# Four chained layers on one core: layer 0's settling by quarters of the tokens, and the end of layer 2 beside the start of layer 3

## The chip, the core and the metric

The kernel runs on one core of a Trainium2 chip. A core has five engines that work side by side and wait for each other by semaphores: TensorE (PE in the profile, with its weight loads listed apart as PEld), which multiplies matrices into the PSUM memory; VectorE (DVE), for arithmetic over rows and reductions; ScalarE (ACT), for functions such as Exp, Tanh and Gelu, of which it holds some in a table and has to load another table for others; GpSimd (POOL); and SyncE (SP), which here only issues DMA transfers. Each engine works through its own queue in the order in which the program puts it. On-chip memory is SBUF, 128 partitions wide.

The metric is the device time of one execution in microseconds (us).

## The reference

The input is x, 8 sequences of 512 tokens with 128 features (f32). Four layers follow, and each is

```
xn = layernorm(x)
s  = attention_i(xn, ...)
g  = silu(ffn_i(xn, ...))
x  = x + s * g
```

Layer 0's "attention" is a recurrence with 16 heads of 8 features. Per token it updates an 8x8 state S for each head, reads y from it, and normalizes y over the 8 features of the head:

```
S = S*exp(w)[:, None] + (S @ kk)[:, None]*b + v[:, None]*k ;  y = S @ r
yn = (y - mean(y)) / sqrt(var(y) + 0.00064) * ln_w + ln_b
out = ((yn + (sum(r*k*faaaa))*v) * g) @ output.T
```

Its ffn is a mixture of 48 experts, each of which takes its 128 best tokens. Layer 1 is an attention over a Taylor feature map with a mixture of 8 experts. Layer 2 has causal softmax attention (16 heads), then eight steps of a small recurrence over the whole sequence,

```
u = tanh(ctx @ w_ctx + xs @ w_x + b);  vn = vs + 0.1*(u - xs - vs);  xs = xs + 0.1*vn
```

then a Gelu block, and a separate gated ffn of width 512. Layer 3's "attention" is a state-space mixer: parameters (decays, rotations, mixing weights) from a projection, and then chunks of tokens in order. Its ffn slot holds an attention with 16 heads whose softmax goes over the queries, followed by two normalized projections.

## The kernel before

A tile holds 128 rows (P). A sequence of 512 tokens has JT = 4 token tiles, and there are B = 8 sequences. `blocks` runs `layer0` to `layer3` one after the other, and x stays in SBUF throughout. Python generators express work that is spread among other work: each `yield` ends a piece, and whoever holds the generator calls `next` to emit the next piece.

**Who sets the order.** By default a planner orders each engine's instructions by estimated readiness, in favour of what comes first in the program. `manual_schedule(engines=...)` takes engines out of its hands: they get their instructions exactly as the program emits them. Layers 0, 1 and 2 do so for PE alone, layer 3 for PE, DVE, ACT and POOL. Memory comes from tile pools. A tile whose memory was used by an earlier one waits until that one's last user is done.

**Layer 0.** For each of the four token tiles (`jt`), the partitions hold the 128 pairs of sequence and head, and the recurrence goes over the 128 tokens two at a time: 64 pairs of tokens, in 8 rounds of SH = 8 pairs (`o`). A round emits, in this order: an expert piece from `side`, three pieces of the next token tile's preparation (`go_on(3)`), the outputs of the round before (`outputs`: sums over 8 values on PE by `eighths` and an ACT copy into Y), another expert piece, two more pieces of preparation, and then the recurrence itself (L734 to L765), nearly all of it DVE instructions of 32 to 128 columns in two interleaved halves. After the eight rounds comes the settling for the whole token tile (L772 to L782): DVE adds the part of v that the pairing left out (L772, L773); the mean over 8 values is formed by `eighths` on PE, and DVE subtracts it (L777); ACT squares (L778); PE sums the squares; ACT takes Ln and Exp for the inverse root (L779, L780); DVE forms the bonus times v (L781) and scales Y (L782). Then ACT applies ln_w and ln_b (L784, eight instructions), PE adds and transposes (L796), DVE applies the gate (L799), and the output projection follows (L804 to L814).

**Layer 2.** It loops over 128 units (sequence, head group, key tile): weights (scores and Exp), maxima for later units, and the sums of LAG = 2 units before. Between these, `fill` emits pieces of the next sequence's start (`begin`, `ffn`), and of the finished sequences (`group`, `rest`). `group` turns the sums into outputs, and its last call for a sequence also does the output projection. `rest` does the norm, the eight recurrence steps (L1557 product with w_x, L1559 add, L1560 Tanh, L1562 to L1565 updates), and the Gelu block, and adds into x (L1603). When the loop ends, the last sequence's pieces remain, and the last two lines of `layer2` emit them with nothing beside them.

**Layer 3.** `begin(b)` normalizes a sequence and projects queries, keys and values for the ffn slot's attention, and then goes on into `parameters`, for the mixer. After `begin(0)`, up to its values, a loop goes over 8 x 16 units plus an end. A unit has `scores` (PE products L2089 into four PSUM banks, DVE maxima L2091, ACT exponentials L2094; a bank is free for the next unit once its exponential is done), `weigh` for two units before (L2119), `scale` for the unit before (the reciprocal L2105), and two calls of `fill`. `fill` gives one piece to every active mixer, and to ends and begins as long as a credit (SHARE a call) lasts. A mixer handles one token tile of one sequence (its first product is L1978). Unit `at(b, jt)` starts it: every 3 units from unit 9 on, and later every 4. If the sequence's parameters aren't complete by then, they are emitted all at once. `end(b)` does the projections behind the attention and the final sum, and issues the output DMA.

Of the kernel before, what the change touches and what calls it, by code (L numbers as in the profile page):

```python
# [20 lines left out]
P = 128  # L21
B = 8
# [308 lines left out]
def layer0(k, x, A, at):  # L331
# [5 lines left out]
    with ExitStack() as ctx:  # L337
# [355 lines left out]
        for jt in range(JT):  # L693
# [12 lines left out]
            yp = Y.rearrange("p (t s) v -> p t s v", s=2)  # L706
            last = None
            for o in range(0, HT, SH):
                if jt == JT - 1 and o // SH >= HT // SH - JT:
# [13 lines left out]
                    else:  # L723
                        held = f, old
                next(side, None)
                go_on(3)
                if last:
                    outputs(*last)
                next(side, None)
# [38 lines left out]
            outputs(*last)  # L768
            go_on(40)
            ready = made  # L770
            t3 = fp.tile([P, B, C], F32, name="EWt").rearrange("p b (h n) -> p (b h) n", n=8)
            nc.vector.tensor_tensor(t3[:, 0:HT], Vs[:, :, 0, :], bc(kr, 2, 8), ALU.mult)  # L772
            nc.vector.tensor_tensor(yp[:, :, 0, :], yp[:, :, 0, :], t3[:, 0:HT], ALU.add)  # L773


            mu = bp.tile([P, P], F32, name="mu")
            nc.vector.scalar_tensor_tensor(Y, Y, 8.0, bc(eighths(Y), 2, 8), ALU.mult, ALU.subtract)  # L777
            nc.scalar.activation(t3, Y, AF.Square)  # L778
            nc.scalar.activation(mu, eighths(t3), AF.Ln, bias=k.eps_gn, scale=1.0 / 8)  # L779
            nc.scalar.activation(mu, mu, AF.Exp, scale=-0.5)  # L780
            nc.vector.tensor_tensor(t3, Vs.rearrange("p t s n -> p (t s) n"), bc(bonus, 2, 8), ALU.mult)  # L781
            nc.vector.tensor_tensor(Y, Y, bc(mu, 2, 8), ALU.mult)  # L782
            for n in range(8):
                nc.scalar.activation(  # L784
                    Y[:, :, n], Y[:, :, n], AF.Identity, scale=cn["ln_w"][:, n : n + 1], bias=cn["ln_b"][:, n : n + 1]
                )

# [4 lines left out]
            for n0 in range(0, 8, 4):  # L792
                ps = k.pa((P, 4, P))
                for i in range(4):
                    for src in (Y, t3):
                        nc.tensor.matmul(  # L796
                            ps[:, i, :], src[:, :, n0 + i], k.ident, start=(src is Y), stop=(src is t3)
                        )
# [515 lines left out]
class Layer2(BySequence):  # L1314


    def __init__(self, k, ctx, x, A, at):
        self.k, self.x = k, x
        nc, tc = k.nc, k.tc
        pool = lambda name, bufs=1: ctx.enter_context(tc.tile_pool(name="l2" + name, bufs=bufs, reuse_waits="tile"))  # L1320
        cp = pool("c")
        self.cn = cn = k.load_consts(cp, A["c2"], at[0], "c2")
        self.fn = fn = k.load_consts(cp, A["f2"], at[1], "f2")

        self.half_s = cp.tile([P, 4], F32, name="half_s")
        nc.vector.tensor_scalar(self.half_s, fn["w1_s"], 0.5, None, ALU.mult)
        self.both_s = cp.tile([P, 4], F32, name="both_s")
# [279 lines left out]
def layer2(k, x, A, at):  # L1607

    with ExitStack() as ctx:
# [62 lines left out]
        for _ in chain(groups, rest):  # L1672
            next(front, None)
# [644 lines left out]
```

## Time and profile before

| | us |
|---|---|
| median of three runs (3601.0 to 3603.7) | 3602.8 |
| the profiled execution's own time | 3603.7 |
| its span, from first to last instruction | 3602.0 |
| layer 0's last update of x | 875.3 |
| layer 2's loop: first score | 1466.4 |
| layer 3's loop: first score | 2624.5 |

How to read the profile: a line of a stretch gives its start, end and length in us; then for PE, PEld, DVE, ACT and POOL the busy us and, in brackets, the number of instructions; then the clock that PE was granted (1 is full), the DMA engines' busy share and GB/s. A stretch for one source line has only the engine of that line. A line of the timeline gives start and duration in us, engine, line, operation, output and inputs, their shapes, and how often; in square brackets stands how long the engine had been idle, and for whom it waited. Neighbouring instructions of one kind are merged, and the duration then runs from the first's start to the last's end. An f32 product appears as two MATMUL passes, each with its own weight load.

### The profile page before, as it was taken

The numbers are of one execution on the slowest core, as the hardware profiler recorded it, in microseconds if no ns is written. First come the engines' busy times: TensorE is split into PE (matmuls) and PEld (weight loads), VectorE is DVE, ScalarE is ACT, GpSimd is POOL, SyncE is SP. The second block draws the span as 40 slices with busy tenths as digits, with TensorE's granted clock in tenths as the row PEclk, the third lists the DMA queues.
The fourth block names the chain that finished last, engine by engine and source line by source line (L and its number), as shares of the span: only waits on it lengthen the run. The fifth ranks groups of instructions, "written<-read, shape, count | busy, mean of one in ns | idle before, by whom it ended". The sixth has DMA issues, their size and how long they took to land.

```text
span 3602.0 us, 46273 instructions
## 1 busy us (share of the span) xinstructions
PE 2864.4 (80%) x16950; PEld 1575.1 (44%) x16950; DVE 2322.8 (64%) x6354; ACT 1790.3 (50%) x3382; POOL 729.9 (20%) x845
## 2 busy tenths in 40 slices
PE   6175868635988898798888898898588798888887
PEld 4154656534444454333334333443235454444443
DVE  7999888896582334435455454554368777777775
ACT  4173646412544455254454554455255565666665
POOL 0012131300225553101111111111112221212221
PEclk8587889766899999899999999999678888888888
DMA  4012121211001222000000000000000000000000
GB/s 121 2 30 44 31 52 32 43 49 34 1 13 37 39 42 47 37 1 1 1 1 1 1 1 1 1 1 1 2 20 1 4 4 3 2 4 4 4 1 7
DMA packets 67523, 64.59 MB, mean 18 GB/s; under 512 B 5344, under 2 KB 59616, under 8 KB 66784
## 3 DMA queue, kind: packets, MB, share of 16 engines
q1 hardware_dynamic: 39264, 42.75, 3.9%
q0 software_dynamic: 19712, 14.69, 3.1%
q10 hardware_dynamic: 8320, 4.19, 0.4%
q8 instruction: 133, 2.18, 0.3%
q14 instruction: 94, 0.77, 0.1%
HBM read 43.80 MB, written 17.83 MB: 17 GB/s over the span
## 4 chain that ended last, share of the span: by engine, by line
PE 34%; DVE 14%; ACT 10%; issue 2%; POOL 1%; DMA 0%; POOLq 0%; ACTq 0%; DVEq 0%; SPq 0%
PE pu L1454 6%; PE ph L1435 5%; PE pu L2089 5%; DVE nm L2091 2%; PE pf L2119 2%; ACT at L2094 2%; PE pf L1503 2%; ACT at L1490 2%; ACT L1490 1%; PE pa L1557 1%; DVE mpad L1469 1%; PE pu L1466 1%; PE pa L1580 1%; PE pa L2132 1%; PE pa L2027 1%
## 5 line engine op out<-in xcount | busy, mean ns | idle before, releaser
L2094 ACT ACTIVATE at<-pu,nm 128x512 f32<-128x512 f32 x512 | 348.0, 691 | 195.9 <-DVE nm L2091 193.4
L2091 DVE TENSOR_REDUCE nm<-pu 128x1 f32<-128x512 f32 x512 | 319.0, 682 | 90.7 <-PE pu L2089 90.6
L2089 PE MATMUL pu<-qT,kT 32*128 32x512 f32 x1024 | 285.8, 732 | 87.6 <-ACT at L2094 87.2
L199 POOL TENSOR_SCALAR_AFFINE_SELECT at<-at 128x512 f32<-128x512 f32 x184 | 125.1, 680 | 1024.4 <-ACT at L1490 878.0
L1469 DVE TENSOR_REDUCE mpad<-pu 128x2 f32<-128x1024 f32 (+3 forms) x256 | 199.0, 819 | 148.8 <-PE pu L1466 148.7
L1128 ACT ACTIVATE at<-pu,rsqrt 128x1024 f32<-128x1024 f32 (+3 forms) x256 | 191.1, 793 | 188.0 <-PE pu L1123 160.7
L1435 PE MATMUL ph<-hid,f 128*128 128x512 f32 x512 | 255.5, 626 | 11.6 <-ACT hid L1436 11.5
L1490 ACT ACTIVATE at<-pu 128x1024 f32<-128x1024 f32 (+3 forms) x256 | 167.0, 701 | 163.7 <-PE pu L1454 162.7
L364 PE MATMUL pa<-HR,ident 128*128 128x128 f32 x512 | 127.8, 418 | 140.2 <-DVE HR L765 140.2
L364 PEld LDWEIGHTS pa<-HR,ident 128*128 128x128 f32 x512 | 112.7, 265 | 150.2 <-DVE HR L765 74.6
L2089 PEld LDWEIGHTS pu<-qT,kT 32*128 32x128 f32 x1024 | 95.3, 212 | 177.9 <-ACT at L2094 162.5
L2119 PE MATMUL pf<-at,va 128*32 128x512 f32 x1024 | 165.0, 723 | 1.9 <-POOL va L2106 1.9
L608 POOL DMA_INDIRECT f_d<-ys,idx x48 | 87.8, 1828 | 384.6 <-ACT ys L607 355.1
L1454 PE MATMUL pu<-kT,qT 32*128 32x512 f32 (+3 forms) x1024 | 134.9, 500 | 30.0 <-ACT at L1490 29.2
L1454 PE MATMUL pu<-qT,kT 32*128 32x512 f32 (+3 forms) x1024 | 128.0, 492 | 20.7 <-DVE mpad L1469 20.2
L1435 PEld LDWEIGHTS ph<-hid,f 128*128 128x128 f32 x512 | 94.1, 198 | 113.2 <-issue 89.2
L2106 POOL TENSOR_TENSOR va<-V,sm 128x32 f32<-128x32 f32 x128 | 33.7, 263 | 489.0 <-DVE sm L2105 488.4
L1123 PE MATMUL pu<-qT,kT 32*128 32x512 f32 (+3 forms) x1024 | 128.4, 507 | 5.3 <-ACT at L1128 4.4
L1066 POOL DMA_INDIRECT f_d<-ys,idx x64 | 102.8, 1606 | 142.7 <-DMA f_d<-ys,idx 86.0
L1490 ACT ACT_TABLE_LOAD x66 | 84.7, 1283 | 87.8 <-PE pu L1454 87.0
L1133 DVE TENSOR_TENSOR at<-at,ceiling 128x512 f32<-128x512 f32 x72 | 49.9, 695 | 105.6 <-ACT at L1128 99.9
L691 ACT COPY Y<-pa 128x128 f32<-128x128 f32 x32 | 8.5, 265 | 208.7 <-PE pa L364 208.7
(621 smaller groups left out, 6772.5 us busy)
## 6 DMA issues: line engine op xcount, KB each, us to landing
w<-in_w_dram SPq DMA_DIRECT2D x24, 512.0 KB
f_d<-zeros ACTq DMA_DIRECT2D x8, 512.0 KB
xn_d<-xn SPq DMA_DIRECT2D x8, 512.0 KB
w<-in_w_dram SPq DMA_DIRECT2D x16, 256.0 KB
w<-in_w_dram SPq DMA_DIRECT2D x24, 128.0 KB
f<-in_f_dram SPq DMA_DIRECT2D x1, 2888.0 KB
xn<-in_x_dram SPq DMA_DIRECT2D x4, 512.0 KB
Gt<-in_x_dram SPq DMA_DIRECT2D x4, 512.0 KB
```

Source lines behind the costliest of these rows:

```text
L199: self.nc.gpsimd.affine_select(a, a if src is None else src, pattern, ALU.is_ge, 0.0, base=0, channel_multiplier=-1)
L364: nc.tensor.matmul(ps, k.ident, src[:, :, i], start=(i == 0), stop=(i == 7))
L1123: nc.tensor.matmul(pu[:, n, 0:m], q["kT"][r, g // 2, kc * P : kc * P + P], q["qT"][r, g, kc * P :], start=True, stop=True,)
L1128: nc.scalar.activation(at_[:, i : i + 2, 0:m], pu[:, :, 0:m], AF.Square, bias=k.rsqrt2, scale=32.0**-0.5)
L1435: nc.tensor.matmul(ps, fn[n][:, c0 : c0 + P], src[:, i, :], start=(i == 0), stop=(i == 3))
L1454: self.k.nc.tensor.matmul(pu[:, n, 0:m], a[r, c0 : c0 + P], b[r, q0 : q0 + m], start=True, stop=stop)
L1469: nc.vector.tensor_reduce(top[:, i : i + 2, 16 + g % 2], pu[:, :, 0:m], AX.X, ALU.max)
L1490: nc.scalar.activation(at_[:, i : i + 2, 0:m], pu[:, :, 0:m], AF.Exp, scale=8.0**-0.5)
L2089: nc.tensor.matmul(pu, q["kT"][r, kc * P : (kc + 1) * P], q["qT"][r, g, :], start=True, stop=True)
L2091: nc.vector.tensor_reduce(nm[:, n : n + 1], pu, AX.X, ALU.max, negate=True)
L2094: nc.scalar.activation(E[:, n, :], pu, AF.Exp, bias=nm[:, w], accum_out=sm[:, w])
L2119: nc.tensor.matmul(po[i * 32 : i * 32 + 32, :], va[:, kc, c0 : c0 + 32], E[:, i, :], start=(kc == 0), stop=(kc == JT - 1))
```

## The change

In layer 0 the settling, up to the scaling of Y, becomes a generator `settle(c)` for a quarter of the tokens (16 pairs, 32 tokens). Quarter c starts in the third, fifth or seventh round (c = 0, 1, 2), right after the outputs of the round before, and gives one further piece at the start of each later round. The fourth quarter, and what is left of the third, are emitted after the rounds. The bonus times v now overwrites Vs, where it had its own buffer. The ln_w scaling and all that follows stay as they were.

In layers 2 and 3, `layer2` no longer emits the last sequence's remaining pieces. It leaves them in `k.tail` with a function that frees their memory. Layer 2's pools split for this: what the tail needs (constants c2, small tiles, work tiles) lies on the right side of SBUF and stays; the ffn's weights, values, queries, keys and weights lie on the left side and are freed before layer 3. Layer 3 emits one tail piece after each piece of `begin(0)`, then one after the first half of each unit's scores, and one more at the end of every odd unit, all in its fixed order. `parameters` is separate from `begin`, with a list of its own; `parameters(0)` starts once the tail is done. Mixers start from unit 19 every 10/3 units. SHARE is 1.9. Ends come last in `fill`, one at a time, and their first projection, now `attended(b)`, is emitted with the last `weigh`. Layer 3's pools use the same `reuse_waits="tile"` as the others.

```diff
+            def settle(c, Y=Y, yp=yp, mu=mu, Vs=Vs, bonus=bonus, kr=kr):
+                pr, tk = slice(c * 16, c * 16 + 16), slice(c * 32, c * 32 + 32)
+                own_v = bp.tile([P, 16, 8], F32, name="own_v")
+                nc.vector.tensor_tensor(own_v, Vs[:, pr, 0, :], bc(kr[:, pr], 2, 8), ALU.mult)
+                nc.vector.tensor_tensor(yp[:, pr, 0, :], yp[:, pr, 0, :], own_v, ALU.add)
+                yield
+                y = Y[:, tk, :]
+                nc.vector.scalar_tensor_tensor(y, y, 8.0, bc(eighths(y), 2, 8), ALU.mult, ALU.subtract)
+                square = bp.tile([P, 32, 8], F32, name="square")
+                nc.scalar.activation(square, y, AF.Square)
+                v = Vs.rearrange("p t s n -> p (t s) n")[:, tk, :]
+                nc.vector.tensor_tensor(v, v, bc(bonus[:, tk], 2, 8), ALU.mult)
+                yield
+                nc.scalar.activation(mu[:, tk], eighths(square), AF.Ln, bias=k.eps_gn, scale=1.0 / 8)
+                nc.scalar.activation(mu[:, tk], mu[:, tk], AF.Exp, scale=-0.5)
+                nc.vector.tensor_tensor(y, y, bc(mu[:, tk], 2, 8), ALU.mult)
+                yield
+
+            settling = []
...
+                for works in settling:
+                    next(works, None)
                 next(side, None)
                 go_on(3)
                 if last:
                     outputs(*last)
+                    if o // SH % 2 == 0:
+                        settling.append(settle(o // SH // 2 - 1))
+                        next(settling[-1])
...
             outputs(*last)
+            settling.append(settle(3))
             go_on(40)
             ready = made
-            t3 = fp.tile([P, B, C], F32, name="EWt").rearrange("p b (h n) -> p (b h) n", n=8)
-            nc.vector.tensor_tensor(t3[:, 0:HT], Vs[:, :, 0, :], bc(kr, 2, 8), ALU.mult)
-            nc.vector.tensor_tensor(yp[:, :, 0, :], yp[:, :, 0, :], t3[:, 0:HT], ALU.add)
...
-            nc.vector.scalar_tensor_tensor(Y, Y, 8.0, bc(eighths(Y), 2, 8), ALU.mult, ALU.subtract)
-            nc.scalar.activation(t3, Y, AF.Square)
-            nc.scalar.activation(mu, eighths(t3), AF.Ln, bias=k.eps_gn, scale=1.0 / 8)
-            nc.scalar.activation(mu, mu, AF.Exp, scale=-0.5)
-            nc.vector.tensor_tensor(t3, Vs.rearrange("p t s n -> p (t s) n"), bc(bonus, 2, 8), ALU.mult)
-            nc.vector.tensor_tensor(Y, Y, bc(mu, 2, 8), ALU.mult)
+            for step in chain(*settling):
+                pass
...
 def layer2(k, x, A, at):
+    late = ExitStack()
...
-        for _ in chain(groups, rest):
-            next(front, None)
+        assert next(front, None) is None
+        k.tail = chain(groups, rest), late.close
...
 def layer3(k, x, A, at):
...
-        SHARE = 1.75
-        EARLY, EVERY = 9, 3
-        at = lambda b, jt: max(b * U + jt * JT - 2, EARLY + EVERY * (b * JT + jt))
-        mixers, begins, ends = [], [L.begin(0)], []
-        while not L.q or "ready" not in L.q[0]:
-            next(begins[0])
+        SHARE = 1.9
+        EARLY, EVERY = 19, 10 / 3
+        at = lambda b, jt: max(b * U + jt * JT - 2, EARLY + int(EVERY * (b * JT + jt)))
+        mixers, begins, parameters, ends = [], [], [], []
+        tail, release = k.tail
+        for _ in L.begin(0):
+            next(tail, None)
...
-            for works in (mixers, ends, begins):
-                for w in works[:1] if works is begins else list(works):
+            for works in (mixers, begins, parameters, ends):
+                for w in list(works) if works is mixers else works[:1]:
...
+                if b and n == b * U - 1:
+                    whole(begins)
+                if b and n == max((b - 1) * U + 8, at(b - 1, JT - 1) + 1 - U, at(b - 2, JT - 1) + 1 if b > 1 else 0):
+                    while "V" not in L.q.get(b, ()):
+                        next(begins[0])
+                    parameters.append(L.parameters(b))
             scores = L.scores(*divmod(n, U)) if n < B * U else iter(())
             next(scores, None)
+            if tail and next(tail, False) is False:
+                tail = None
+                release()
+                L.more_pools()
+                parameters.append(L.parameters(0))
             fill()
             next(scores, None)
             if LAG <= n < B * U + LAG:
-                L.weigh(*divmod(n - LAG, U))
+                b, u = divmod(n - LAG, U)
+                L.weigh(b, u)
+                if u == U - 1:
+                    assert not tail
+                    L.attended(b)
+                    ends.append(L.end(b))
             if 1 <= n <= B * U:
                 L.scale(*divmod(n - 1, U))
+            if tail and n % 2:
+                next(tail, None)
             fill()
```

## The prediction

> **What bounds the kernel now.** I read the page first, then a table of stretches, then the timeline of the two seams that the change touches. The page:
>
> ```profile
> span 3602.0 us, 46273 instructions
> ...
> DVE  7999888896582334435455454554368777777775
> ...
> PEclk8587889766899999899999999999678888888888
> ```
>
> A slice is 90 us. In layer 0 (slices 3 to 9) VectorE (DVE) is at 9 of 10: the recurrence is a chain on it. In layers 1 and 2 TensorE (PE) is the busy engine. At slice 29, the seam from layer 2 to 3, DVE and the granted clock both dip. The stretches (busy us of PE, PEld, DVE, ACT and POOL, then the clock):
>
> ```profile
> 708.00:839.00 131.00, 50.82 (x227) 46.04 (x227) 121.55 (x680) 22.26 (x39) 7.22 (x8) 0.64 0.14 34
> 839.00:875.30 36.30, 24.72 (x104) 22.61 (x104) 9.49 (x13) 11.19 (x17) 3.64 (x7) 0.68 0.02 2
> 2470.00:2544.00 74.00, 61.09 (x352) 28.33 (x350) 31.14 (x51) 41.72 (x53) 9.28 (x13) 0.93 0.00 1
> 2544.00:2624.50 80.50, 39.51 (x108) 17.74 (x108) 33.00 (x59) 14.02 (x21) 8.06 (x9) 0.64 0.06 23
> 2690.60:2960.60 270.00, 232.32 (x1323) 134.12 (x1322) 209.41 (x467) 162.82 (x432) 67.13 (x98) 0.87 0.01 3
> 2960.60:3546.70 586.10, 503.85 (x2733) 265.85 (x2733) 443.89 (x1018) 367.57 (x966) 125.88 (x197) 0.85 0.01 3
> ```
>
> Row 1 is layer 0's last token tile: DVE does 121.6 of 131 us, so a DVE instruction put there costs its own time. Row 2 is what follows it, 36 us in which no engine is full. Row 4 is the tail of layer 2's last sequence: 80.5 us of pure latency from its last sums to layer 3's first score. The timeline shows one of its eight recurrence steps:
>
> ```profile
> 2564.22 0.69 DVE L1565 SCALAR_TENSOR_TENSOR X<-X,u 128x512 f32<-128x512 f32 x1 [0.79 <-ACT u L1560]
> 2564.94 0.69 DVE L1564 SCALAR_TENSOR_TENSOR X<-X,X 128x512 f32<-128x512 f32 x1
> 2564.96 0.50 PEld L1557 LDWEIGHTS pa<-X,c 128*128 128x128 f32 x2 [3.84 <-DVE X L1565]
> 2564.96 2.08 PE L1557 MATMUL pa<-X,c 128*128 128x512 f32 x2 [2.26 <-DVE X L1565]
> 2567.08 0.69 DVE L1559 TENSOR_TENSOR u<-pa,cw 128x512 f32<-128x512 f32 x1 [1.44 <-PE pa L1557]
> 2567.86 0.72 ACT L1560 ACTIVATE u<-u,c 128x512 f32<-128x512 f32 x1 [3.68 <-DVE u L1559]
> ```
>
> One step is 4.40 us (2564.96 to 2569.36), of which every engine is free for half or more.
>
> Layer 3 is a loop over 128 units (one head group against one key tile), in an order that the program fixes on four engines. One reciprocal (L2105) per unit counts them:
>
> ```profile
> 2690.60:2960.60 270.00, 5.57 (x33) 0.87 0.01 3
> 2960.60:3546.70 586.10, 13.34 (x79) 0.85 0.01 3
> ```
>
> The first stretch holds 33 units and 11 mixers (one every 3 units; counted by L1978, two passes each), the second 79 units and 20 mixers (one every 4). If a unit costs b and a mixer with its share of begin, parameters and end costs m: 33b + 11m = 270.0 and 79b + 20m = 586.1, so b = 5.0 and m = 9.5 us. This pair carries the sum below.
>
> **Layer 0, the settling by quarters.** Removed per token tile: five DVE instructions, 2 x 0.69 (128x512) + 3 x 1.23 (128x1024) = 5.1 us. Added: 20, per quarter two of 128x128 and three of 128x256. The nearest rows are 0.29 (L1522) and 0.42 (L1593): 1.84 a quarter, 7.4 a tile, +2.3. Back to back, starts lie closer than durations (two of 128x64 in 0.35, not 2 x 0.22), which makes the difference +1.0; I take +1.6. TensorE's two sums over the eight values become eight of a quarter of the columns; each still loads weights 16 times, 3.66 to 3.77 us at the low clock, so about 3.7 instead of 4.1 each. PE's 80 idle us of row 1 cover the 22 us that a tile gains (eight of 3.7 less two of 4.1); if PE is late, DVE waits at each sum. POOL and SP get nothing here. ACT gets four times the Ln and Exp. The last tile's end:
>
> ```profile
> 844.21 4.12 PE L364 MATMUL pa<-Y,ident 128*128 128x128 f32 x16 [1.08 <-DVE Y L773]
> 848.36 1.22 DVE L777 SCALAR_TENSOR_TENSOR Y<-Y,pa 128x1024 f32<-128x1024 f32 x1 [4.21 <-PE pa L364]
> 850.75 1.28 ACT L779 ACT_TABLE_LOAD   x1
> 850.78 4.00 PE L364 MATMUL pa<-EWt,ident 128*128 128x128 f32 x16 [2.46 <-ACT EWt L778]
> 855.21 1.28 ACT L780 ACT_TABLE_LOAD   x1
> ```
>
> Here row and rule differ. The Trainium skill's "ScalarE: Activation LUTs" (Table sets: the hidden batching unit) says that a logarithm followed by an exponential needs one table load, since one set has both, and (What ACT_TABLE_LOAD costs) that a switch is 2.66 us, load and drain. The trace has two loads, of 1.28 each, with Exp starting 0.01 us after the second. By the rule a quarter pays one switch of 2.66 us, and 5.3 with the way back to Gelu or Tanh, and the exposed end would lose 1.3 us. I go by the row: 2 x 1.28 a quarter and one load back, 3.8 us. ACT is idle 109 us of row 1; earlier tiles have it half busy, and there a late Ln can push the next tile's front.
>
> Inner tiles (three): +1.6 of DVE; the two DVE waits for the sums (L777 2.03, L781 2.03 at 361 and 368) lose one, since the bonus product no longer overwrites the squares, -2.0; new waits of DVE on PE or ACT inside the recurrence, unseen before, bounded by none and by two of 2.0 per quarter: I take +1.0. That is +0.6 each, +1.8. Last tile: three quarters inside its full DVE, at 1.4 us with overlap, +4.2. Its end from 843.5 to 858.1 shrinks: add 0.69 to 0.29, sums 8.1 to 7.4, subtraction 1.22 to 0.42, square 1.06 to 0.4, scale 1.23 to 0.42, -3.7 with the smaller Ln and Exp; but the third quarter's variance sum now stands before it on PE, 3.7 less the 1.1 that PE idled there: +2.6. The eight ACT scalings and what follows stay. So -1.1, and layer 0 is +1.8 + 4.2 - 1.1 = **+5 us** (from -8, all six waits gone and no new one, to +18, one more wait of 2 us per quarter in half of them).
>
> **Layer 2 into layer 3.** The layer 2 loop keeps its order; its tiles only change place. Its first loads may go earlier or later than 1435 and 1443 us, but what ends last there is the sum into x on POOL (to 1447.6): 0, within 3.
>
> The start of layer 3. Its constants (1313 and 514 KB) fall where layer 2's ffn weights lay, last read at about 2520; their 7 us (issue 2609.8, first use 2616.8) end before 2544, SP being idle. If an overlap delays them past 2544, each us counts. begin(0) took 14.5 us by itself (2610.0 to 2624.5). Now its nine pieces alternate with nine of the tail: four that finish the attention, the norm, X, and three recurrence steps. Before, those reached 2571.5. The tail leads, and begin's two 2-us products, Wk and Wq, and two qT scalings of 0.75 fall into it, while a busier PE shortens the product from 2.08 to the 1.12 that it had at 2509.5. I put the first scores at 2569 instead of 2624.5: **-55.5**.
>
> The first eight units. Twelve calls remain, 1.5 a unit. A unit with a step runs: scores 0.6, four maxima 2.5, u 0.7, Tanh 0.8, two exponentials 1.4, hand-overs 0.5, some 6.5; a second step adds some 3 to 4; the last norm adds 6, the two Gelu pieces 4 each with 2 x 1.28 of loads, begin(1) some 5. Summed: 5.5 + 12 + 6 + 12 + 5 + 11 + 5.5 + 7.5 = 65. Bare they would be 40. What is late behind the tail on ACT are the unit's third and fourth exponentials, on PE the next scores that need their banks.
>
> The rule that speaks against this is in "TensorE: Matmul & The Clock Gate" (Architectural detail): ScalarE's and VectorE's queues are strictly first in, first out. Read at its hardest, each of the 12 calls adds its whole latency: 8 x 5.0 + 12 x 4.4 = 93 us. The trace agrees in kind: at 2672 the parameters' sine waits 0.77 and loads tables twice around a unit's exponentials, and that unit takes 7.5. But most of a step's 4.4 passes while DVE does the unit's maxima. I take 65 and keep 93 for the range.
>
> The rest. Units 8 to 18: parameters(0), moved here, at the 6.2 us that nine units had with it before (2635.3 to 2690.8): 68. Units 19 to 121 hold 31 mixers, one per 10/3 units: 103 x 5.0 + 31 x 9.5 = 811 (7.9 a unit). The end was 55.3 and gets 3, as the sixth end now yields to parameters. Sum 65 + 68 + 811 + 58 = 1002, against 2624.5 to 3602.0, 977.5: **+24.5**. The larger share and the moved pieces add no instruction; the output DMAs stay on SP.
>
> **Sum.** -55.5 + 24.5 + 5 = -26. The profiled execution took 3603.7 (span 3602.0), 0.9 above the median of 3602.8 of the runs shown; so 3577.7 for it, and **3577** against the median.
>
> **Rivals.**
> A. Denser mixers don't add up. One every 3 units ran at 270/33 = 8.18 a unit, and 16 of them (2736.6 to 2881.0) at 9.0. It decides at 7.9 + 26/103 = 8.15. At 8.3, 103 units are 855: +44, **3621**. For it: the strict order. Against it: the 8.18 held three sets of parameters pushed through at once, which the later start avoids.
> B. The strict queues at their hardest: +28, **3605**, about no change.
> C. Spacing costs nothing, 7.46 a unit as from 3011 on (119.4 us per 16): 768, -43, **3534**.
> D. Layer 0 stalls, +18 in place of +5: **3590**.
> E. The overlap fails: layer 3's first tiles wait for memory that the tail holds, as L1821 waited 1.30 us for POOL's last addition. The start stays (+55.5) and the eight units are bare (-25): **3607**. The tail's pools on the right side speak against it.
>
> **How the numbers follow.** Forecast 0.47, A 0.11, B 0.12, C 0.18, D 0.08, E 0.04. Range 3540 to 3610: it holds all but A and half of C. Faster by over 0.2% (7.2 us, about what a measurement of this kernel can tell) means under 3595.6: forecast, C, D and a third of B, 0.77. Same: most of B and E, 0.11. Slower: A and the rest, 0.12.
>
> **What would show it.** First score near 2569, after a layer 0 that ends 5 us later; w_x products among scores; eight units in 65; 103 units at 7.9; DVE in layer 0 with more instructions and waits on L364. It is wrong if the first score stays past 2590 or the units with mixers exceed 8.15.

## The result, and the profile after

The changed kernel takes **3632.1 us** (median of four, 3628.6 to 3636.7) where the kernel before, run beside it, takes 3603.3: a ratio of **1.0077, interval 1.0065 to 1.0089**. It is slower by 29 us. The forecast was 3577, and the range up to 3610 doesn't hold the result. The profiled execution took 3633.9. Two executions among the runs below took 4420 and 6057 us, far from all others of their kernels, and the medians leave them out.

First the page of the changed kernel, the same rows that the prediction shows of before:

```profile
span 3632.2 us, 47167 instructions
...
DVE  7989787877575333624554554554477677777776
...
PEclk9587888855789999899999999999888888877888
```

Two things differ. In layer 0 (slices 3 to 9) DVE went 9988889 and now goes 8978787, and PE's clock falls from 6 to 5 in slices 9 and 10. At the seam from layer 2 to layer 3 (slice 29) the clock no longer dips to 6, and DVE dips to 4 and not to 3. Layer 0 lost time, and the seam gained some.

Where layer 0's recurrence ends can be read from its last instruction per round (L765 before, L793 after). The columns are the count, shortest, median and longest duration in ns, and the first and last start in us. Before:

```profile
L765 DVE TENSOR_TENSOR HR<-Hs,Rs x32: 679/691/729, 214.4 to 838.2; 128x512 f32<-128x512 f32 x32
L814 DVE TENSOR_TENSOR x<-sg,Gt x2: 691/691/691, 871.9 to 874.6; 128x512 f32<-128x512 f32 x2
```

After:

```profile
L793 DVE TENSOR_TENSOR HR<-Hs,Rs x32: 679/692/693, 213.3 to 885.2; 128x512 f32<-128x512 f32 x32
L834 DVE TENSOR_TENSOR x<-sg,Gt x2: 692/693/694, 915.4 to 919.0; 128x512 f32<-128x512 f32 x2
```

The recurrence ends **47.0 us later**, with the same 32 rounds of the same duration. What follows it is 2.6 us shorter (33.8 in place of 36.4), so layer 0 is 44.4 us longer in all. All four token tiles lost time: 10.6, 7.4, 11.3 and 17.7 us in their order. The stretches of the changed kernel, in the prediction's columns (busy us of PE, PEld, DVE, ACT and POOL, then the clock), show the last token tile of layer 0, the stretch up to layer 3's first score, and layer 3's loop cut at units 8, 19 and 122 and at the end:

```profile
731.20:885.20 154.00, 71.47 (x339) 66.64 (x339) 127.71 (x716) 32.08 (x55) 6.17 (x8) 0.54 0.12 29
2544.00:2616.20 72.20, 51.35 (x275) 26.63 (x274) 30.50 (x55) 30.52 (x42) 10.46 (x14) 0.84 0.07 27
2616.20:2683.50 67.30, 54.39 (x196) 21.03 (x195) 43.87 (x77) 40.71 (x88) 4.89 (x11) 0.74 0.00 0
2683.50:2749.90 66.40, 56.26 (x273) 26.10 (x270) 47.66 (x124) 42.55 (x115) 8.44 (x18) 0.85 0.00 1
2749.90:3577.60 827.70, 729.51 (x3835) 397.75 (x3833) 621.39 (x1428) 500.27 (x1315) 189.41 (x281) 0.84 0.01 3
3577.60:3632.20 54.60, 36.80 (x242) 21.68 (x242) 29.95 (x60) 26.68 (x68) 7.62 (x13) 0.86 0.02 6
```

The second row begins where the prediction's row of the tail did, but all is later here: layer 2's last sums start at 2584.7. From there to layer 3's first score it is 31.5 us, where it was 80.8 before (2543.7 to 2624.5).

The last token tile, from the end of the recurrence before it to its own, takes 154.0 us with 127.7 us of DVE work. Cut in the same way (701.9 to 838.2), it took 136.3 with 126.5 before: 1 us more work in this tile, and 17 us more of standing still. Over the whole recurrence (186 us to its end) DVE is busy 588.5 us after and 584.8 before: of the 47 us, 4 are work and 43 are waiting. The groups of instructions name the waits; they are taken to 878 us before and to 925 after, and so include what the last tile does behind its recurrence. Layer 0's settling and gate, before (busy us and mean ns, then idle time of the engine just ahead of them and what ended it):

```profile
L799 DVE TENSOR_TENSOR Rt<-pa,Gt 128x512 f32<-128x512 f32 x8 | 8.6, 1074 | 13.3 <-PE pa L796 13.3
L781 DVE TENSOR_TENSOR EWt<-Vs,bonus 128x1024 f32<-128x1024 f32 x4 | 4.9, 1225 | 11.4 <-PE pa L364 11.4
L777 DVE SCALAR_TENSOR_TENSOR Y<-Y,pa 128x1024 f32<-128x1024 f32 x4 | 4.9, 1221 | 10.3 <-PE pa L364 10.3
L782 DVE TENSOR_TENSOR Y<-Y,mu 128x1024 f32<-128x1024 f32 x4 | 4.9, 1220 | 0.7 <-ACT mu L780 0.7
L773 DVE TENSOR_TENSOR Y<-Y,EWt 128x512 f32<-128x512 f32 x4 | 2.8, 692 | 5.6 <-ACT Y L691 5.6
```

And after:

```profile
L819 DVE TENSOR_TENSOR Rt<-pa,Gt 128x512 f32<-128x512 f32 x8 | 8.6, 1074 | 18.3 <-PE pa L816 18.3
L726 DVE TENSOR_TENSOR Y<-Y,mu 128x256 f32<-128x256 f32 x16 | 6.8, 425 | 43.8 <-ACT mu L725 34.6 <-issue 9.2
L718 DVE SCALAR_TENSOR_TENSOR Y<-Y,pa 128x256 f32<-128x256 f32 x16 | 6.7, 418 | 23.1 <-PE pa L364 23.0
L715 DVE TENSOR_TENSOR Y<-Y,own_v 128x128 f32<-128x128 f32 x16 | 4.6, 290 | 11.1 <-ACT Y L691 11.1
```

The sixteen scalings by mu (L726) work 6.8 us and wait 43.8 us; in the kernel before, the four scalings waited 0.7 us. (For 9.2 of the 43.8 the profile names no releaser.) The subtraction (L718) waits 23.1 in place of 10.3. L781's 11.4 us are gone, as the prediction said. Up to the end of the recurrence alone, L726 and L718 wait 34.7 and 23.1 us; before, L777 and L781 waited 6.1 each and L782 not at all. The timeline of one such place, in the last tile:

```profile
840.68 3.53 PEld L364 LDWEIGHTS pa<-square,ident 128*128 128x128 f32 x16
840.91 3.43 PE L364 MATMUL pa<-square,ident 128*128 128x32 f32 x16
...
841.41 1.28 ACT L724 ACT_TABLE_LOAD   x1
841.57 0.18 DVE L787 TENSOR_TENSOR Hs<-Z 128x32 f32<-128x32 f32 x1
844.38 0.29 ACT L724 ACTIVATE mu<-pa,eps_gn 128x32 f32<-128x32 f32 x1 [1.69 <-PE pa L364]
844.68 1.28 ACT L725 ACT_TABLE_LOAD   x1
845.98 0.23 ACT L725 ACTIVATE mu<-mu 128x32 f32<-128x32 f32 x1
846.24 0.42 DVE L726 TENSOR_TENSOR Y<-Y,mu 128x256 f32<-128x256 f32 x1 [4.49 <-ACT mu L725]
846.58 0.18 DVE L787 TENSOR_TENSOR Hs<-Z 128x32 f32<-128x32 f32 x1
```

DVE does one half of a recurrence step (L787) at 841.57. The next instruction in its queue is the scaling L726. Its input comes out of a chain that has only begun: sums on PE until 844.34, Ln, a table load, Exp until 846.21. DVE stands for 4.49 us, and the other half of the same step, which needed nothing, starts at 846.58.

### The profile page after: what moved, and what is told of

It reads as the page before. It is cut to its first block, busy times and chain, and to the rows that moved or that the text cites. A ratio compares the mean times of both kernels' runs of the same rounds, so it can differ in the third digit from the quotient of the medians.

```text
span 3632.2 us, 47167 instructions
## 1 busy us (share of the span) xinstructions
PE 2941.1 (81%) x17334; PEld 1650.3 (45%) x17334; DVE 2324.4 (64%) x6414; ACT 1837.8 (51%) x3451; POOL 724.0 (20%) x845
## 4 chain that ended last, share of the span: by engine, by line
PE 36%; DVE 13%; ACT 10%; issue 2%; POOL 1%; DMA 0%; POOLq 0%; ACTq 0%; DVEq 0%
PE pu L1482 5%; PE ph L1463 5%; PE pu L2122 5%; PE pf L2152 2%; DVE nm L2124 2%; ACT at L2127 2%; PE pf L1531 2%; ACT at L1518 2%; ACT L1518 1%; DVE mpad L1497 1%; PE pa L1585 1%; PE pa L2165 1%; PE pu L1494 1%; PE pa L2054 1%; PE pa L1616 1%
## 5 line engine op out<-in xcount | busy, mean ns | idle before, releaser
L2122 PE MATMUL pu<-qT,kT 32*128 32x512 f32 x1024 | 294.2, 739 | 77.9 <-ACT at L2127 77.7
L1143 PE MATMUL pu<-qT,kT 32*128 32x512 f32 (+3 forms) x1024 | 127.7, 505 | 5.2 <-ACT at L1148 4.4
```

Of the source, the lines that this page charges most:

```text
L1143: nc.tensor.matmul(pu[:, n, 0:m], q["kT"][r, g // 2, kc * P : kc * P + P], q["qT"][r, g, kc * P :], start=True, stop=True,)
L2122: nc.tensor.matmul(pu, q["kT"][r, kc * P : (kc + 1) * P], q["qT"][r, g, :], start=True, stop=True)
```

## Experiments: the two halves apart

**Layers 2 and 3 alone.** Layer 0 is the one before, everything from layer 2's class on is the changed one.

> Layer 0 as before, layers 2 and 3 as changed. If the two parts are independent, as the traces of before and after suggest (start of layer 3 55 us earlier, its loop 38.5 us longer), this takes 3603 - 17 = 3586 us: faster than both. If the end of layer 2 and the start of layer 3 were slowed by something that layer 0 left behind (the clock, memory places), the loop of layer 3 is shorter than 1016 us from its first score, and the time nearer to the 3577 that was forecast.

Measured: 3593.5 us median beside 3605.8 of before (ratio 0.996, interval 0.9944 to 0.9976), some 7 above the 3586 expected; its profiled execution took 3591.3. It is faster than both kernels. The first score came at 2572.5, 52 us earlier than before, and the loop then took 1017.1 us, as in the changed kernel (1016.0). So the loop is not disturbed by layer 0, and it is longer than the 1002 forecast whatever layer 0 does.

**Layer 0 alone.** The reverse.

> Layer 0 settled by quarters, layers 2 and 3 as before. With independent parts: last update of the recurrence at about 885 instead of 838 us, and 3603 + 46 = 3649 us. If the 47 us of layer 0 are partly given back later (loads of layer 1 or 2 that have more time to land), less: under 3640.

Measured: 3649.5 us median (1.0121, 1.0104 to 1.0138), the recurrence ending at 881.7, as expected. Nothing of it is given back later: layer 3's loop takes 978.7 us. The two halves, -12.3 and +43.7 us, add up to +31; the change measured +29.

## Experiments on layer 0

Layers 1 and 2 stand between layer 0 and the end, and take 1720 to 1736 us from the recurrence's end to layer 3's first score in the various runs of the changed kind. So these experiments are read at the end of the recurrence, 838.2 before and 885.2 after, from one profile each. Five profiles with the settling of before end it at 834.7 to 838.2, and the two with the changed one at 881.7 and 885.2: a difference of under 4 us is not read as one.

**A round later in the program.**

```
-  nc.vector.scalar_tensor_tensor(y, y, 8.0, bc(eighths(y), 2, 8), ALU.mult, ALU.subtract)
+  nc.scalar.copy(mu[:, tk], eighths(y))
+  yield
+  nc.vector.scalar_tensor_tensor(y, y, 8.0, bc(mu[:, tk], 2, 8), ALU.mult, ALU.subtract)
...
   nc.scalar.activation(mu[:, tk], mu[:, tk], AF.Exp, scale=-0.5)
+  yield
   nc.vector.tensor_tensor(y, y, bc(mu[:, tk], 2, 8), ALU.mult)
```

> The changed kernel with the same work per quarter, but the two DVE instructions that follow TensorE or ScalarE (subtraction of the mean, scaling by mu) are put into the next round of the recurrence, a round after the sums and functions that they need; the mean waits in SBUF, for which ScalarE makes one more copy of 128x32. Theory 1 (DVE works in order, and the planner put these two at a point where their inputs weren't there yet, so that the recurrence behind them stood still): their waits inside the recurrence, some 34 of scaling and 23 of subtraction, mostly go, and the recurrence ends 30 to 45 us earlier, 3590 to 3602 us. Theory 2 (the added work itself, table loads on ScalarE and sums on TensorE, delays what the recurrence needs from them): the work is the same or more, and the time stays at 3625 to 3640.

Measured: 3640.2 us, the recurrence ending at 887.6. Read by the number alone, theory 2 wins. The timeline shows that the edit didn't do what it was meant to do:

```profile
338.34 0.18 DVE L790 TENSOR_TENSOR Hs<-Z 128x32 f32<-128x32 f32 x1
...
340.37 1.28 ACT L727 ACT_TABLE_LOAD   x1
341.66 0.23 ACT L727 ACTIVATE mu<-mu 128x32 f32<-128x32 f32 x1
341.92 0.43 DVE L729 TENSOR_TENSOR Y<-Y,mu 128x256 f32<-128x256 f32 x1 [3.40 <-ACT mu L727]
342.26 0.18 DVE L790 TENSOR_TENSOR Hs<-Z 128x32 f32<-128x32 f32 x1
```

This scaling (L729 here, of the second quarter) is emitted behind the tile's eighth round, and it stands on DVE between the two halves of one step of the seventh. DVE's order in this layer is the planner's, by estimated readiness; it drew the instruction forward, to 3.40 us before mu was ready. Over the recurrence the scalings wait 35.1 us, where they wait 34.7 in the changed kernel. The run says nothing on the theories.

**Subtraction and scaling on POOL.** POOL is busy 128 of 699 us in this stretch. The two instructions go there from the three-piece form of the changed kernel.

```
+  nc.scalar.activation(mu[:, tk], eighths(y), AF.Copy, scale=1.0 / 8)
+  nc.gpsimd.tensor_tensor(y, y, bc(mu[:, tk], 2, 8), ALU.subtract)
...
+  nc.gpsimd.tensor_tensor(y, y, bc(mu[:, tk], 2, 8), ALU.mult)
```

> The changed kernel with the subtraction of the mean and the scaling by mu on POOL, not DVE (ScalarE copies the mean, already divided by 8, out of PSUM; eps goes with it). Sums, Ln, Exp and table loads stay. The deferred version left the order to the planner, which drew the two instructions back into the middle of the recurrence, so that it didn't settle theory 1; here nothing of the recurrence can stand behind them on DVE. Theory 1 (DVE's own queue behind these two): DVE's waits inside the recurrence drop by 45 to 57 us, its busy time by 32 x 0.43 = 14 us, the recurrence ends at 825 to 845 us, and the whole takes 3575 to 3595. Theory 2 (added work on ScalarE and TensorE delays what the recurrence needs): the recurrence still ends later than 865, and the whole takes over 3612.

Measured: 3615.9 us beside 3595.8 of before (1.0056, 1.0036 to 1.0075), the recurrence ending at 862.7. That is 22.5 us back, about half, between the two expectations. The groups show where the rest went:

```profile
L820 DVE TENSOR_TENSOR Rt<-pa,Gt 128x512 f32<-128x512 f32 x8 | 8.6, 1075 | 52.7 <-PE pa L817 52.7
L715 DVE TENSOR_TENSOR Y<-Y,own_v 128x128 f32<-128x128 f32 x16 | 4.6, 290 | 13.0 <-ACT Y L691 13.0
```

The two waits are gone from DVE, and the next instruction behind the same chain, the gate (L820), waits 52.7 us in place of 18.3: about 10 us at each seam of two tiles, with the next tile's recurrence behind it. DVE's busy time didn't fall by 14 us either: 588.3. The recurrence's additions (L786, L788) and products (L782) are slow where they overlap one of the two instructions on POOL: L786 takes 401 ns on average in these 15 cases and 216 in the other 497, L782 443 and 217, L788 452 and 186. The reductions (L780) take 210 and 209. Over the recurrence this adds up to some 9 us of DVE.

**The same without Ln and Exp**, the inverse root by a power on POOL:

```
-  nc.scalar.activation(mu[:, tk], eighths(square), AF.Ln, bias=k.eps_gn, scale=1.0 / 8)
-  nc.scalar.activation(mu[:, tk], mu[:, tk], AF.Exp, scale=-0.5)
+  nc.scalar.activation(mu[:, tk], eighths(square), AF.Identity, bias=k.eps_gn, scale=1.0 / 8)
+  nc.gpsimd.tensor_tensor(mu[:, tk], mu[:, tk], k.minus_half.to_broadcast([P, 32]), ALU.pow)
```

> As the last one, but without Ln and Exp and their table loads: ScalarE adds eps and divides (Identity), POOL forms the inverse root by a power of -0.5. By the rows of 128x4 and 128x8 (1.02 and 1.71 us) a power of 128x32 takes some 5 to 6 us of POOL. Theory 2, table loads: ScalarE is relieved of some 60 us of loads over the four tiles, and the recurrence ends 10 us or more earlier than with POOL alone. Theory 1: within 6 us of it, since what DVE waited for was the chain and not ScalarE's time; the last tile's exposed end may be 3 to 6 us longer by the slow power.

Measured: 3627.9 us, the recurrence ending at 880.9, and 18.2 to 18.5 us of waiting for the gate at each seam. Both expectations missed. A power of 128x32 takes 5.58 us on POOL, more than the two loads that it replaces, and the chain in front of the gate became longer. ScalarE was relieved (298 us busy, not 348) and that gained nothing. The wait at the gate follows the length of the chain.

**Taking the waits away.** Three kernels keep the instructions of DVE and take away what they wait for. In the first, subtraction and scaling take `bonus` in place of the mean and of mu:

```
-  ... bc(eighths(y), 2, 8), ALU.mult, ALU.subtract)
+  sums = eighths(y)
+  ... bc(bonus[:, tk], 2, 8), ALU.mult, ALU.subtract)
...
-  nc.vector.tensor_tensor(y, y, bc(mu[:, tk], 2, 8), ALU.mult)
+  nc.vector.tensor_tensor(y, y, bc(bonus[:, tk], 2, 8), ALU.mult)
```

> The changed kernel with every instruction kept, but the subtraction and the scaling take bonus in place of the mean and of mu, so that they wait for no sum and no function (the normalization is thereby left out of the result; sums, squares, Ln, Exp and table loads still run on their engines). Theory 1 (what costs the 47 us is that DVE stands in these waits, in the recurrence and at the seams of the tiles): the recurrence ends at 835 to 848 us. Theory 2 (the added work on ScalarE and TensorE): it ends at 870 to 885. In between, both count.

> As the last one for the first three quarters of a token tile only (their normalization is left out); the fourth, which is settled after the rounds, waits as in the changed kernel. The difference to the last run is what the seams cost. From the waits in the trace (5.3 for the subtraction at three seams and 1.1 to 2.7 for scalings): about 15 to 20 us more than the last run; 5 us or less if the seams cost no more than those of before.

> As the first of these three, and Ln and Exp are left out as well, with their table loads (3.8 us and 0.5 us of ScalarE per quarter, some 60 to 70 us in all). Theory 2: the recurrence ends at least 8 us earlier than there. Theory 1: within 4 us of it, since ScalarE has the room.

Measured ends of the recurrence: **859.3** for all four quarters, **868.8** for the first three, **862.4** without Ln and Exp. So waiting for the mean and mu costs 25.9 us of the 47, of which 9.5 belong to the fourth quarter at the seams (15 to 20 were expected, or at most 5). Leaving out Ln, Exp and all their loads on top gains nothing (the end moves by 3.1 us, within what equal code differs by, and ScalarE's busy time falls from 346 to 293): theory 2 falls as far as table loads go. But 859.3 lies between the ranges of both theories; theory 1 had said 835 to 848. The groups of the first of the three show why the end was not reached:

```profile
L820 DVE TENSOR_TENSOR Rt<-pa,Gt 128x512 f32<-128x512 f32 x8 | 8.6, 1075 | 31.1 <-PE pa L817 31.1
L719 DVE SCALAR_TENSOR_TENSOR Y<-Y,bonus 128x256 f32<-128x256 f32 x16 | 6.8, 423 | 20.2 <-PE pa L364 20.0
L727 DVE TENSOR_TENSOR Y<-Y,bonus 128x256 f32<-128x256 f32 x16 | 6.7, 416 | 0.5 <-ACT square L721 0.5
```

The scaling (L727) waits 0.5 us. The subtraction (L719) still waits 20.2, nearly all for PE: it needs no sum, but it overwrites Y, which PE's sum reads. What was left could be the sums on PE or the added DVE instructions themselves.

**Without the sums.** All DVE instructions stay; the two sums per quarter, the squares, Ln and Exp are left out.

> The changed kernel with all DVE instructions of the quarters kept (subtraction and scaling take bonus), but without their sums on TensorE, squares, Ln and Exp: mean, variance and normalization are left out of the result. The run without Ln and Exp still ended its recurrence at 862.4 us, 24 later than before, with DVE waiting 20 us for TensorE at the subtraction (it may overwrite Y only after the sum has read it) and 18 at the gate. If TensorE's added sums (some 48 us more busy, eight of 2 to 3.7 us a tile) cause that rest, the recurrence ends at 835 to 848. If the added DVE instructions and the places that the planner gives them cause it, it stays at 853 or later.

Measured: the recurrence ends at **833.9**, just below the first of the two ranges, and the whole takes 3570.4 beside 3598.7 of before. Its groups and its stretch:

```profile
L718 DVE SCALAR_TENSOR_TENSOR Y<-Y,bonus 128x256 f32<-128x256 f32 x16 | 6.7, 419 | 0.0
L722 DVE TENSOR_TENSOR Y<-Y,bonus 128x256 f32<-128x256 f32 x16 | 6.7, 419 | 0.0
...
186.00:833.90 647.90, 409.22 (x2482) 334.96 (x2482) 587.72 (x2980) 289.83 (x598) 143.60 (x96) 0.78 0.18 39
```

DVE has the same instructions and the same busy time as in the changed kernel (587.7 against 588.5) and doesn't wait at them. So the added DVE work costs nothing that shows, and the 47 us are waiting for a chain on other engines. From 885.2 to 833.9 it is 51.3 us: 25.9 for the end of the chain (the mean and mu), the rest for its sums on PE, the squares on ScalarE and what these hold up (28.5 from the run without Ln and Exp). The lower clock of PE is in this rest, and no run sets it apart. This run also lacks the sums that the kernel before has at its seams, so it is a lower bound and not the cost of an ideal settling.

**The third quarter out of the seam**, on the POOL version: each quarter's first two pieces are emitted together.

```
   next(settling[-1])
+  next(settling[-1])
```

> As the kernel with subtraction and scaling on POOL, with each quarter begun two pieces at once, so that the third quarter is settled within the rounds and only the fourth is left for the seam of the tiles. There DVE waited 10.0 to 10.6 us for the gate at each of three seams, and the recurrence ended at 862.7. If the two quarters one after the other make up that wait, it falls to 4 to 7 and the recurrence ends at 845 to 855. If it is the chain of the fourth quarter alone (its sums, two table loads, scalings, sums), the wait stays over 8 and the end within 5 us of 862.

Measured: the gate waits 9.9 to 10.3 us as before, and the recurrence ends at 873.1, ten later than in the POOL version. The expectation of a gain was wrong: the fourth quarter's own chain sets the wait at the seam, and the sums, standing earlier on PE, moved waits onto L715 (12.0 us up to the end, from 8.5) and onto the next tile's preparation (L479: 11.0 us, from 1.0).

| kernel | last round of the recurrence, us |
|---|---|
| before | 838.2 |
| changed | 885.2 |
| a round later in the program | 887.6 |
| two instructions on POOL | 862.7 |
| the same, pieces together | 873.1 |
| the same, power for Ln and Exp | 880.9 |
| no wait for mean or mu | 859.3 |
| no wait, first three quarters | 868.8 |
| no wait, no Ln and Exp | 862.4 |
| no sums, no Ln and Exp | 833.9 |

## Experiments on layer 3's loop

The loop took 1016.0 us where 1002 was forecast. It repeats: ten profiles that hold the changed loop (the changed kernel, its variants in layer 0, layers 2 and 3 alone) have 1013.6 to 1019.6, the two with the loop of before 977.5 and 978.7. Three runs change the pacing.

**One number of the kernel with only layers 2 and 3 changed**: `EARLY, EVERY = 19, 3` in place of `19, 10 / 3`.

> As the kernel with only the parts of layers 2 and 3, but mixers start from unit 19 every 3 units and from unit 82 on every 4, in place of every 10/3. If units and mixers add up (5.0 and 9.5 us), the pacing is worth nothing: the same time as that kernel within 4 us. If a mixer costs more when they stand denser (rival A), the dense units go at 8.4 or more and the ones with four between at 7.5, and the sum is within 5 us too, but uneven. If it is the spacing of 10/3 that doesn't fit the unit's rhythm of four key tiles, the stretch with every fourth unit falls back to 119.4 us per 16 units and the time is 10 to 20 us shorter.

Measured: 3605.7 us beside 3605.8 (1.0001, 0.9991 to 1.0011); the loop takes 1032.4, 15 us longer. No expectation had that. The stretch with one mixer per four units takes 125.3 to 125.8 us per 16 units, where the same spacing had 119.4 before.

**The order and share of before**: SHARE 1.75, and ends ahead of begins, all at once.

> Layer 0 as before and the parts of layers 2 and 3, but with the share of before (1.75, not 1.9) and the order of before between the works of a unit: ends ahead of begins, all of them at once, not last and one at a time. The spacing stays at 10/3. If what the loop of layer 3 lost (units 16 to 112 at 8.13 us, where 5.0 + 0.3 x 9.5 = 7.85 was expected) comes from that order, it gets 10 to 25 us back and takes 3565 to 3582. If it comes from the spacing of the mixers and the clock (rival A), it stays within 6 us of 3590.

Measured: 3592.5 beside 3595.8 (0.9995, 0.9985 to 1.0004), and a loop of 1022.6: no gain, as rival A's side of the expectation had it. Neither the order of `fill` nor the share is the cause.

**The kernel before with the other spacing**: `EARLY, EVERY = 9, 10 / 3`.

> The kernel before with one number changed: mixers start every 10/3 units from unit 9 on, not every 3 (units 9 to 62; later one every 4 as before). If units and mixers add up (5.0 and 9.5 us), the loop of layer 3 takes the same within 4 us, 977. Rival A (mixers standing denser than one in 4, or out of step with the units' groups of four, cost more): the stretch of 10/3 goes at 8.1 to 8.3 a unit; as the dense stretch before had 8.2 to 9, the sum is then the same or up to 10 us shorter, and the stretch with one in 4 keeps its 119.4 us per 16 units.

Measured: a loop of 994.5 against 977.5, **17 us longer from the spacing alone**. (The whole took 3607.3 beside 3601.5, one execution each: layers 0 to 2, the same code, ended 13.5 us earlier in this one.) Units 9 to 62 go at 8.35, against 8.16, a little above the 8.1 to 8.3 of rival A, and no sum that I expected came out 17 longer. Units 19 to 62, before:

```profile
2747.90:3109.20 361.30, 301.17 (x1656) 168.04 (x1648) 278.19 (x636) 214.28 (x561) 81.67 (x120) 0.85 0.01 3
```

And with the spacing of 10/3:

```profile
2732.50:3105.80 373.30, 307.86 (x1660) 174.76 (x1659) 276.59 (x639) 216.71 (x565) 81.82 (x120) 0.82 0.01 3
```

The same instructions within some missing records, the same busy time of DVE, ACT and POOL, and 12 us more: PE is busy 6.7 us longer for the same matmuls, at a granted clock of 0.82 in place of 0.85, and idle 5 us more. Another 7 us are lost behind unit 62, and 2 gained ahead of unit 19. So a unit and a mixer don't have fixed prices: how they fall beside each other counts. That it does so through PE's pauses and its clock is a reading, not shown. The spacing also moves the units at which parameters that aren't complete are emitted all at once, and no run holds these fixed. Over five arrangements of the loop (the time at half clock is summed from the clock records of each trace):

| loop of layer 3 | length | us of it at half clock |
|---|---|---|
| before: one in 3, then one in 4, from unit 9 | 977.5 | 302 |
| before, one in 10/3 from unit 9 | 994.5 | 340 |
| changed: one in 10/3 from unit 19 | 1016.0 | 337 |
| layers 2 and 3 changed, order of before | 1022.6 | 333 |
| layers 2 and 3 changed, one in 3, then 4, from unit 19 | 1032.4 | 372 |

The first two have the same work, and so do the last three among each other. Within both groups the slowest has the most time at half clock, but the other two of the last group don't follow it, and the second profile of before's loop has 313 us at half clock at 1.2 us more length. So the clock can be a part of it at most.

## Why the prediction was wrong, by its own steps

**Layer 0: the step that failed.** The sum had +5 and the trace shows +44.4: 39 of the 56 us by which the whole sum was off. The term is the new waits of DVE inside the recurrence, taken at +1.0 an inner tile; the two waits in its place took 57.8 us in all, where those of before took 12.2. In detail:

- *DVE work*, +1.6 per inner tile and +4.2 in the last, 9 in all: 4 us measured, 1 of it in the last tile, and the run without sums shows that these instructions find room. Right in kind, and too high.
- *The wait at L781 that goes*, -2.0 per inner tile: the three were 6.1 us (the fourth tile's lies behind the recurrence), and they are gone. Right.
- *"new waits of DVE on PE or ACT inside the recurrence ... I take +1.0"*: this is the term. Up to the end of the recurrence L726 and L718 wait 57.8 us, 14.4 a tile; before, L777 and L781 waited 12.2, or 3 a tile. The working bounded the new waits by two of 2.0 per quarter, which is 16 a tile, and then took 1.0 without a row that spoke for it. Carried into the sum (16 in each inner tile, 12 for the three quarters in the last), its own upper end was about +62 for layer 0 and not +18 (there it had become one wait of 2 us in half of the quarters). The range missed the result at this place and at no other.
- *The size of one wait*, 2.0 from L777 and L781: those rows wait for sums alone. The new chain has sums of 1.9 to 3.6 us, two loads of 1.28, Ln and Exp. The prediction had all of these numbers, counted them as ScalarE's load and found ScalarE idle. They are latency, and DVE's queue stood behind it.
- *"PE's 80 idle us of row 1 cover the 22 us"*: PE had the room, and DVE still waited for the end of each sum. In the last tile PE's clock fell from 0.64 to 0.54, and a sum of sixteen weight loads took 3.43 us, where others in the layer take 1.88 (those starting at 277.4 and 664.3).
- *Rival D* ("layer 0 stalls") named the mechanism. Its +18 was the wrong size, and its 0.08 the wrong chance.
- *"a DVE instruction put there costs its own time"* (the reading of row 1): the run without sums has the three quarters' DVE work and ends its recurrence no later than before.
- *The exposed end*: -1.1 forecast, -2.6 measured.
- *The rule on table loads* ("ScalarE: Activation LUTs", one load for Ln and Exp) was weighed against the row and set aside; the changed kernel loads twice per quarter, 1.28 each, as the row said. Once DVE doesn't wait for mu, leaving them out gains nothing that can be read.

**Start of layer 3.** The first score was forecast at 2569 with a layer 0 as before: 2616.2 less 44.4 is 2571.8, and with the old layer 0 it came at 2572.5. The gain of 55.5 is 52 to 53, 49 of it between layer 2's last sums and the first score. Right.

**The first eight units.** 65 forecast; from the first unit's maxima (2618.4) to the ninth's (2683.5) it is 65.1. Rival B, the queues at their hardest (93), is excluded. Units 8 to 19 were forecast at 68 and took 66.4.

**Units 19 to 122.** 811 forecast, **827.7** measured, 8.04 a unit and not 7.9. That lies between the forecast and the 8.15 from which rival A decides. The term that was off is the pair b = 5.0 and m = 9.5, solved from two stretches and taken as fixed prices. The kernel before at this spacing shows that they are not; why stays open.

**The end.** 58 forecast, 54.6 measured. The loop is 14 us longer than the 1002 of the sum.

**The sum.** -52.7 at the start of layer 3, +38.5 in its loop and +44.4 in layer 0 make +30.2, the difference of the two spans. With +5 in layer 0 it would have been about -9, which is near what the kernel with only layers 2 and 3 changed shows. The better version is that one: the settling as it was, the end of layer 2 beside layer 3, 0.996 of the time before.

## What to carry to other kernels

Before you move a short dependent chain from behind a chain that fills an engine to inside it, add up its latency over all engines and put it against the place where its consumer will stand in the full engine's queue: room on the other engines is no cover for an engine that works in order. Where a planner sets that place by an estimate, emitting the consumer later in the program doesn't move it; look at the timeline to see where it landed. And a cost that is bounded from two sides belongs in the range with its upper end as it was derived, not with a milder one.

## What was not expected of the hardware

Leaving out Ln, Exp and their table loads, 53 us of ScalarE's busy time, didn't bring the recurrence's end forward (859.3 with them, 862.4 without) where DVE didn't wait for their result. ScalarE had the room here, 346 us busy of 673.

The small additions and products on DVE, which read two inputs, take about twice as long beside a subtraction or scaling on POOL: 401 ns in place of 216, 443 of 217 and 452 of 186 on average, and up to 831 in one case. A reduction, which reads one input, takes 210 beside them and 209 elsewhere.

A pause of PE is paid for after it. In the loop of the kernel before, where one mixer starts per four units, PE stands for 7.2 us once in 16 units (at 3104.9, 3224.4, 3343.8 and 3463.3). Each time 13.7 us at half clock begin 3.5 us into the pause. The third of them (stretches ahead of the pause, at half clock, and behind it):

```profile
3337.00:3343.80 6.80, 6.80 (x42) 3.67 (x40) 6.52 (x14) 3.27 (x8) 2.19 (x2) 1.00 0.00 0
3347.30:3361.00 13.70, 10.00 (x34) 4.81 (x34) 9.32 (x22) 9.36 (x25) 0.48 (x2) 0.50 0.00 1
3361.00:3367.00 6.00, 5.64 (x44) 3.13 (x36) 5.32 (x10) 3.97 (x11) 2.60 (x5) 1.00 0.01 3
```

PE stood from 3343.8 to 3351.0; the clock is 0.50 from 3347.3 to 3361.0, although PE is busy without a break for the last 10.0 of these 13.7 us. The Trainium skill ("TensorE: Matmul & The Clock Gate", What's actually happening) describes a gate that closes after an idle window of about 3.4 us and opens after at least one such window of sustained work. The closing agrees. The opening took 10.0 us of work here, nearly three such windows.

The same pieces of the same program, spaced at 10/3 units and not at 3 and 4, cost 17 us more. Why PE stands idle longer at that spacing was not followed through, and stays open.
